# A two-layer graph network in f32: four node tiles instead of six in the first phase, and another place in memory for s of layer 1

## The chip, the cores and the metric

The kernel runs on one core of one Trainium2 chip. The metric is the device time of one execution in microseconds (us). The kernel before takes 2101.34 us, the median of three runs (2098.91 to 2105.48). A core has five engines with an order of instructions each: TensorE (PE, with its weight loads PEld), VectorE (DVE), ScalarE (ACT), GpSimd (POOL) and SyncE (SP). Transfers are issued by SP, ACT and POOL.

## The reference

There are 4096 nodes with 512 features in f32 and one dense matrix `adj` of 4096 × 4096, in which about 0.8% of the entries are not zero. Both layers begin with a layer norm and a relu, and add their result to their input.

```python
# layer 0
h = relu(layernorm(x))
d = where(adj.sum(1) > 0, adj.sum(1) ** -0.5, 0)
x = x + relu((d[:, None] * adj * d[None, :]) @ h @ W0 + b0)
# layer 1
h = relu(layernorm(x))
s, t = (h @ W1) @ a[:512], (h @ W1) @ a[512:]
e = leaky_relu(s + t.T, 0.2)
p, q = softmax(where(adj > 0, e, -1e12)), -softmax(where(adj > 0, -e, -1e12))
x = x + elu(concat(p @ h, q @ h) @ wtrans)
```

## The kernel before

The nodes are cut into 32 tiles of 128. Layer 0 computes `y = d * (h @ W0)` for all tiles (`y0`, kept in memory) and then `adj @ y`, for a few output tiles at a time: a group `(i0, n)` of the list `GROUPS` stands for the n output tiles from i0 on. For each of the 32 row tiles of y, a group needs a block of the transposed matrix, 128 rows × n·128 columns (`at`).

**The first group, (26, 6),** is worked on while y is made. In round j SP issues the four pieces of 512 KB of the rows of adj (`ar`, `load_adj`) and the block `at`. ACT sums three of the pieces and VectorE one (L669, L671), since d needs the sum of a row. POOL issues x, four tiles ahead (L640, five buffers). The layer norm (statistics on VectorE, L433; the root and the scaling on ACT, L632, L636) gives hx (two buffers); TensorE transposes it (L648), multiplies by W0 (yp, L679), and ACT scales by d (L702). Then come n products of 128 × 512 for row tile j (acc, L852), in n PSUM banks that stay occupied for the whole phase; transposes and projections alternate in the banks that are left of the eight. The pattern of non-zeros of the block goes as bytes to the tables of layer 1 (`pack`, L716 to L727). After 32 rounds, and four small products for the attention vectors, the phase is over.

**The later groups** use products of half width, 128 × 256. Two output tiles and two row tiles form a 2 × 2 block, and seven products of sums and differences take the place of eight (`multiply_blocks`, L893). The sums of columns are made by VectorE from `at` (`sum_at`, L880 to L883); the differences of y (`sum_y`, L865 to L868) are made once, in the first of these groups. A group has 16 steps jp. The results of a group are taken out of PSUM at the start of the next (`evict` after the first group, with three extra tiles in `new_y` since it has six rows; `join_blocks` after the others), and its rows are finished there, one in each of the first steps: relu and residual (L808), layer norm (h, L636, two buffers), two dot products with the attention vectors (`prod`, L816), and the row is written to eight tables of layer 1 (`put_row`, L443: one write issued by POOL, seven by ACT, 258 KB each). At step 8, TensorE turns the values s of these rows (`spread_s`, L831), and ACT writes them out. The rows of the last two groups are written to one table and copied to the others later. The order of instructions on each engine comes from a planner; some are pinned to the order of the program. `EARLY` says in which group the masks of the last three are packed, since these must be there when layer 1 begins. The lists of neighbours for layer 1 are made beside the groups (`make_lists`).

**Layer 1** gathers for each pair of tiles the rows of the neighbours from a table (POOL, L451), adds s and t (`scores`, L463), takes the two exponentials, multiplies by the mask (L482), and multiplies (L1296); then comes the product with wtrans (L1319). Its tiles are laid out by pools in the order in which these are opened; what lies where the late products of layer 0 read must wait for them. s is loaded by SP (L1256), wtrans by ACT.

Of the kernel before, what the change touches and what calls it, by code (L numbers as in the profile page):

```python
# [8 lines left out]
F32 = mybir.dt.float32  # L9
# [10 lines left out]
P = 128  # L20
IB = 512


GROUPS = ((26, 6), (16, 4), (20, 4), (0, 4), (4, 4), (8, 4), (12, 4), (24, 2))

EARLY = {(24, 2): (2,), (12, 4): (3,), (8, 4): (4,)}
PAIR0 = 16
Y_PARTS = (8, 11, 13)
T_PARTS = (7, 9)
# [230 lines left out]
def gcn_gat_kernel(  # L260
# [24 lines left out]
    N, F = x.shape  # L285
# [15 lines left out]
    TT = RPT * RB // P  # L301
    late0, n_late = GROUPS[-1]
    tab0 = PAIR0 // TT
# [14 lines left out]
    with sbuf(name="init", bufs=1) as init:  # L318
        column = init.tile([P, P], F32, name="column")
        nc.vector.memset(column[:, 0:1], 0.0)  # L320
        n = 1
# [195 lines left out]
    with sbuf(name="y0", bufs=1) as y_pool, sbuf(name="wa", bufs=1) as wa_pool, sbuf(name="bits", bufs=4) as bits_pool, sbuf(name="small0", bufs=4) as small, ExitStack() as rest, ExitStack() as lists:  # L517
# [16 lines left out]
        keys, lst = {}, {}  # L534
# [214 lines left out]
        def affine(y, acc, j):  # L749

            nc.vector.scalar_tensor_tensor(y, acc, d_all[:, j : j + 1], b_bc, ALU.mult, ALU.add)
            return y

        def new_y(work, j, k):
            if k < 0:
                return work.tile([P, F], F32, tag="y", name=f"y{j}", bufs=4)
            if k == 0:
                spare.append(make_pool.tile([P, 3, F], F32, tag="keys", name="spare"))
            return spare[0][:, k]

        def evict(i0, acc, work, _):

            return {
                i0 + k: affine(new_y(work, i0 + k, k - 3), a, i0 + k) for k, a in enumerate(acc)
            }

        def join_blocks(i0, n, acc, work, new_w):

            ys = {}
            for x in range(n // 2):  # L770
                p16, p23, p45, p7 = acc[x]
                j0, j1 = i0 + x, i0 + n // 2 + x
                ys[j0], ys[j1] = y, v = [new_y(work, j, -1) for j in (j0, j1)]
                w = new_w(f"w{j0}")[:, :H]
                nc.vector.tensor_copy(y[:, :H], p16[:, :H])
                nc.vector.tensor_tensor(w, p16[:, H:], y[:, :H], ALU.add)  # L776
                nc.vector.tensor_tensor(y[:, H:], p45[:, H:], w, ALU.add)

                def first(p23=p23, y=y):
                    nc.vector.tensor_tensor(y, p23, y, ALU.add)  # L780

                def second(p7=p7, w=w, p45=p45, v=v):
                    two = "p (a f) -> p a f"
                    nc.vector.tensor_tensor(w, p7, w, ALU.add)
                    nc.vector.tensor_tensor(
                        v.rearrange(two, a=2),
                        p45.rearrange(two, a=2),
                        w.unsqueeze(1).to_broadcast([P, 2, H]),
                        ALU.add,
                    )  # L790

                if n == 2:
                    first()
                    affine(y, y, j0)
                    second()
                    affine(v, v, j1)
                else:
                    second()
                    first()
            if n > 2:  # L800
                for j, y in ys.items():
                    affine(y, y, j)
            return ys

        def finish0(work, j, y, h, prod):
# [15 lines left out]
            put_row(nc.gpsimd, tab0, j, h)  # L821
            if all(not j0 <= j < j0 + n for j0, n in GROUPS[-2:]):
                for g in others:
# [97 lines left out]
        i0, n = GROUPS[0]  # L921
        with sbuf(name="w0", bufs=1) as w0_pool, sbuf(name="ain", bufs=9) as ain, sbuf(name="xs", bufs=5) as x_pool, sbuf(name="at6", bufs=5) as at_pool, sbuf(name="bits6", bufs=3) as bits6, sbuf(name="ln", bufs=3) as ln_pool:
# [39 lines left out]
            acc = [bank(f"acc{i0 + k}") for k in range(n)]  # L962
            for j in range(NJ):
# [18 lines left out]
                pack(bits6, i0, j, ats.pop(j), j < 2)  # L982
                mark()
        pending = (GROUPS[0], partial(evict, i0, acc))
        listing, joining, spare = [], [], []

        def make_lists(g):
            make_keys(g)

            def rows_and_joins(c):  # L990
                count_listed(g, c, lst[g])
                li = table_rows(g, c, lst[g])
                joining.extend(partial(join, g, li, m) for m in range(c * NE, (c + 1) * NE))
                if c == 2:
                    joining.append(partial(deal, g))

            for n, (c, r) in enumerate(steps):
                listing.append(partial(list_round, keys[g], lst[g], n))
                if n == 5:
                    listing.append(partial(make_places, g))  # L1000
                if r + 1 == CAPS[c] // 8:
                    listing.append(partial(rows_and_joins, c))

        def judge():
# [25 lines left out]
            return verdict  # L1030

        def group(b, work, at_pool, sum_pool, step, prod, n_h=2):

            nonlocal pending
            i0, n = GROUPS[b]
            nj = 8 // n
            (p0, pn), take = pending
            order = [p0 + k for k in ((0, 2, 1, 3) if b > 1 else range(pn))]
            ats, sums = {}, {}

            def prepare(jp):
                if 2 * jp % nj == 0:
                    ats[jp] = load_at(at_pool, i0, n, 2 * jp, nj)
                    sums[jp] = sum_at(sum_pool, ats[jp], n, f"sums{i0}_{jp}")
                else:
                    ats[jp], sums[jp] = ats[jp - 1], sums[jp - 1]
                if b == 1:
                    sum_y(jp)

            prepare(0)  # L1050
            for j in order[:2]:
                if j not in xrs:
                    load_xr(j)
            for jp in range(NP):
                if jp + 1 < NP:
                    prepare(jp + 1)
                mark()
                if jp == 0:
                    ys = take(work, prod)
                    p7 = bank(f"p7_{i0}")  # L1060
                    acc = [
                        [*(bank(f"p{k}_{i0 + x}") for k in (16, 23, 45)), p7[:, x * H : (x + 1) * H]]
                        for x in range(n // 2)
                    ]
                multiply_blocks(acc, n, jp, ats[jp], sums[jp])
                if (i0, n) not in EARLY:
                    pack(bits_pool, i0, 2 * jp, ats[jp])
                for (e0, m), when in EARLY.items():
                    if b in when:
                        pack(bits_pool, e0, 2 * jp, load_at(at_pool, e0, m, 2 * jp, 2))  # L1070
                if jp < pn:
                    j = order[jp]
                    h = work.tile([P, ROW_W], F32, tag="h", name=f"h{j}", bufs=n_h)
                    finish0(work, j, ys.pop(j), h, prod)
                    if jp + 2 < pn:
                        load_xr(order[jp + 2])
                if jp == 8:
                    spread_s(p0, pn)
                if jp == NP - 4:
                    for k in (0, n // 2):  # L1080
                        load_xr(i0 + k)
                step(jp)
            pending = (GROUPS[b], partial(join_blocks, i0, n, acc))

# [5 lines left out]
        make_pool = lists.enter_context(sbuf(name="make", bufs=1))  # L1090
        with sbuf(name="work0", bufs=2) as work, sbuf(name="sums", bufs=3) as sum_pool, sbuf(name="at", bufs=6) as at_pool:

            def prod(name):
                return work.tile([P, F], F32, tag="q", name=name, bufs=1)

            for b in range(1, len(GROUPS) - 1):

                def step(jp):
                    if jp == 2 and b in (3, 5):
                        make_lists((1, 0)[b == 5])  # L1100
                    for _ in range((2, 3)[b == 6] if jp != 2 else 0):
                        if listing:
                            listing.pop(0)()
                    if joining:
                        joining.pop(0)()

                group(b, work, at_pool, sum_pool, step, prod)
            while listing:
                listing.pop(0)()
            while joining:  # L1110
                joining.pop(0)()
# [7 lines left out]
        with sbuf(name="work2", bufs=2) as work, sbuf(name="sums2", bufs=2) as sum_pool, sbuf(name="at2", bufs=4) as at_pool, sbuf(name="scratch", bufs=1) as scratch, sbuf(name="pair", bufs=1) as pair:  # L1119
# [98 lines left out]
            k = late0 % EJ  # L1218
# [17 lines left out]
    def sparse_layer1():  # L1236
        with ExitStack() as pools:

            def pool(name, bufs):
                return pools.enter_context(sbuf(name=name, bufs=bufs))  # L1240
# [2 lines left out]
            slots = ((0, 0), (1, 0), (1, 2), (1, 1), (0, 1), (0, 2))  # L1243
            g_pools = {s: pool("g%d%d" % s, 1) for s in slots}
            tmp, small, p_pool = pool("tmp", 1), pool("small1", 2), pool("p", 3)
            work, ut_pool, wt_pool = pool("work1", 2), pool("ut", 2), pool("wt", 1)
            warm = small.tile([P, 1], F32, tag="warm", name="warm", bufs=1)
            nc.scalar.activation(warm, sign, AF.Exp)
            wt_sb = wt_pool.tile([P, 2 * FC, F], F32, name="wt_sb")
            s_pool = pool("s", 2)  # L1250
            gath, wgt, us, uts, srow = {}, {}, {}, {PAIR0: ut0}, {}

            def load_s(k):
# [82 lines left out]
            order = [r for n in pairs for r in (2 * n, 2 * n + 1)]  # L1336
# [86 lines left out]
```

## Time and profile before

| what | us |
|---|---|
| median of three runs | 2101.34 |
| the profiled execution | 2098.72 |
| its span, first to last instruction | 2096.8 |
| TensorE busy (95% of the span) | 1996.2 |
| VectorE busy (53%) | 1120.1 |
| POOL busy (44%) | 917.0 |
| ACT busy (24%) | 511.3 |
| products of the first phase (acc, L852), 384 records | 174.9 |
| projections (yp, L679), 256 records | 123.2 |
| half-width products of layer 0 (L893), sum of its four rows | 880 |

A record is one entry of the profile; an f32 product shows as two. Busy time counts an engine's instructions without the ones that issue transfers. The mean granted clock of TensorE is 0.981. In the timeline, the first product of the first phase starts at 25.80. The groups start at 334.33 (16, 4), 433.4 (20, 4), 530.6 (0, 4), 637.9 (4, 4), 758.2 (8, 4), 866.0 (12, 4) and 975.1 (24, 2), and the last of them ends at 1030.4. TensorE is busy 200.0 of every 200 us from 1200 to 2000, in layer 1.

### The profile page before, as it was taken

What the parts mean: (1) busy time and instruction counts of PE and PEld (TensorE: products, weight loads), DVE (VectorE), ACT (ScalarE), POOL (GpSimd) and SP (SyncE); (2) the same over time, 40 slices, a digit from 0 to 9 for tenths busy, and PEclk for the clock granted to TensorE, in tenths of its full rate; (3) what the DMA queues carried; (4) which work ended last, traced back from release to release, by engine and by line L of the source; (5) the groups of instructions that cost most, each with busy time, mean ns of one, the idle gap of its engine ahead of it and who ended that gap; (6) DMA issues with size and microseconds to landing.
All of it is one profiled execution on the core that took longest, in us unless ns stands there. A gap on an engine that the chain in (4) does not pass through costs nothing.

```text
span 2096.8 us, 20037 instructions
## 1 busy us (share of the span) xinstructions
PE 1996.2 (95%) x6456; PEld 1180.1 (56%) x6456; DVE 1120.1 (53%) x2805; ACT 511.3 (24%) x876; POOL 917.0 (44%) x980
## 2 busy tenths in 40 slices
PE   7999999999899879899879999999999999999998
PEld 3444446888787768788634444444444444444443
DVE  5444436563798458945545455554544544445441
ACT  4645612222332310000111222212212211121120
POOL 2010001111113320220577777777777777776740
PEclk9999999999999999999989999999999999999999
DMA  9988927887887776383689888888888888888850
GB/s 381 366 307 321 371 71 252 290 284 220 307 281 256 253 222 238 90 270 111 204 265 302 255 288 293 263 287 254 271 240 274 261 258 245 242 247 236 240 161 22
DMA packets 188040, 524.11 MB, mean 250 GB/s; under 512 B 25235, under 2 KB 34419, under 8 KB 187926
## 3 DMA queue, kind: packets, MB, share of 16 engines
q0 software_dynamic: 71296, 275.22, 42.2%
q1 hardware_dynamic: 86640, 192.78, 27.1%
q10 hardware_dynamic: 29990, 54.75, 7.4%
q8 instruction: 52, 0.85, 0.2%
q14 instruction: 62, 0.51, 0.1%
HBM read 430.83 MB, written 102.92 MB: 255 GB/s over the span
## 4 chain that ended last, share of the span: by engine, by line
PE 49%; DVE 6%; DMA 5%; POOL 3%; issue 2%; ACTq 1%; ACT 0%; DVEq 0%; SPq 0%; POOLq 0%
PE u L1296 32%; PE o L1319 10%; PE p L893 5%; POOL g L451 3%; DMA g<-table,idx 2%; DVE keys L393 1%; PE tp L508 1%; DVE lst L391 1%; DMA table<-h 1%; DMA ld<-li,off 1%; DMA at<-in_adj_t 1%; PE u L1174 1%; ACTq L443 1%; DVE prod L816 0%; DMA table<-m 0%
## 5 line engine op out<-in xcount | busy, mean ns | idle before, releaser
L451 POOL DMA_INDIRECT g<-table,idx x704 | 747.8, 1062 | 259.9 <-issue 186.4
L1296 PE MATMUL u<-g,p 128*128 128x512 f32 x1736 | 762.4, 596 | 9.8 <-DVE p L482 9.8
L1296 PEld LDWEIGHTS u<-g,p 128*128 128x128 f32 x1736 | 326.0, 191 | 397.5 <-issue 362.9
L463 DVE TENSOR_TENSOR z<-g,s 128x512 f32<-128x512 f32 (+1 forms) x124 | 77.5, 625 | 390.4 <-DMA g<-table,idx 357.8
L893 PE MATMUL p<-t,sums 128*128 128x256 f32 x832 | 249.0, 384 | 13.3 <-DVE sums L881 13.3
L893 PE MATMUL p<-y,sums 128*128 128x256 f32 x832 | 252.0, 385 | 6.5 <-DVE sums L883 6.5
L893 PE MATMUL p<-y,at 128*128 128x256 f32 x832 | 252.4, 386 | 4.9 <-DMA at<-in_adj_t 4.6
L1319 PE MATMUL o<-wt_sb,ut 128*128 128x512 f32 x512 | 225.1, 592 | 0.5 <-ACT ut L512 0.5
L473 ACT ACTIVATE p<-z 128x896 f32<-128x896 f32 (+2 forms) x136 | 116.1, 905 | 268.3 <-DVE z L469 248.1
L893 PEld LDWEIGHTS p<-t,sums 128*128 128x128 f32 x832 | 159.6, 193 | 37.5 <-DVE sums L881 15.5
L893 PEld LDWEIGHTS p<-y,sums 128*128 128x128 f32 x832 | 160.7, 193 | 29.9 <-DVE sums L883 7.3
L852 PE MATMUL acc<-y,at 128*128 128x512 f32 x384 | 174.9, 593 | 2.4 <-ACT y L702 2.4
L482 DVE SCALAR_TENSOR_TENSOR p<-g,p 128x384 f32<-128x384 uint8 (+1 forms) x256 | 143.2, 620 | 63.3 <-ACT p L473 62.3
L893 PEld LDWEIGHTS p<-y,at 128*128 128x128 f32 x832 | 159.3, 193 | 30.7 <-ACT m L716 5.0
L727 POOL DMA_DIRECT2D table<-m x71 | 54.3, 766 | 248.5 <-ACT m L716 145.5
L1319 PEld LDWEIGHTS o<-wt_sb,ut 128*128 128x128 f32 x512 | 94.8, 190 | 107.8 <-issue 106.9
L716 ACT ACTIVATE m<-at 128x1024 uint8<-128x1024 f32 (+1 forms) x110 | 105.2, 987 | 183.8 <-DMA at<-in_adj_t 137.3
L893 PE MATMUL p<-t,at 128*128 128x256 f32 x416 | 126.3, 386 | 18.5 <-DVE w L776 17.7
L1305 ACT ACTIVATE us<-u,rl 128x512 f32<-128x512 f32 x62 | 42.5, 686 | 414.7 <-issue 217.4
L679 PE MATMUL yp<-w_sb,hx_t 128*128 128x512 f32 x256 | 123.2, 627 | 17.3 <-ACT y L702 14.8
L852 PEld LDWEIGHTS acc<-y,at 128*128 128x128 f32 x384 | 70.5, 190 | 80.5 <-issue 77.4
L413 POOL DMA_INDIRECT ld<-li,off x48 | 43.2, 901 | 159.8 <-DMA ld<-li,off 115.8
(182 smaller groups left out, 1718.5 us busy)
## 6 DMA issues: line engine op xcount, KB each, us to landing
at<-in_adj_t SPq DMA_DIRECT2D x136, 512.0 KB, 5.1
ar<-in_adj SPq DMA_DIRECT2D x128, 512.0 KB, 8.4
table<-h ACTq DMA_DIRECT2D x182, 258.0 KB, 5.8
table<-m POOLq DMA_DIRECT2D x55, 256.0 KB, 5.6
at<-in_adj_t SPq DMA_DIRECT2D x32, 384.0 KB, 5.0
g<-table,idx POOLq DMA_INDIRECT x704, 4.3
xr<-in_x SPq DMA_DIRECT2D x32, 256.0 KB, 3.5
x<-x1d SPq DMA_DIRECT2D x32, 256.0 KB, 5.2
```

The costliest lines, as they stand in the source:

```text
L413: return nc.gpsimd.indirect_dma_start(out=lst_dram[g][:, :], out_offset=bass.IndirectOffsetOnAxis(ap=off[g][:, e, c : c + 1], axis=0), in_ ...
L451: nc.gpsimd.indirect_dma_start(out=gt[:, k, :], out_offset=None, in_=table[2 * n // RPT], in_offset=bass.IndirectOffsetOnAxis(ap=idx[n // ...
L463: return nc.vector.tensor_tensor(z, t.to_broadcast([P, n, RB]), s.unsqueeze(1).to_broadcast([P, n, RB]), ALU.add)
L473: i = nc.scalar.activation(p[:, :, g, :], z, AF.Exp, scale=(1.0, -1.0)[g])
L482: nc.vector.scalar_tensor_tensor(e, m, 0.0, e, ALU.is_gt, ALU.mult)
L679: nc.tensor.matmul(yp, hx_t[j][:, c * P : (c + 1) * P], w0_sb[:, c, :], start=c == 0, stop=c == FC - 1,)
L716: nc.scalar.activation(m, at, AF.Sign)
L727: nc.gpsimd.dma_start(out=rows_of(t, e)[:, c:, ROW_W + (a - t * TT) * P // 4 : ROW_W + (b - t * TT) * P // 4], in_=masks[i0][:, c:, (a - i ...
L852: nc.tensor.matmul(a, at[:, 0, it * P : (it + 1) * P], y0[j], start=j == 0, stop=j == NJ - 1)
L893: i = nc.tensor.matmul(out, left[:, x * P : (x + 1) * P], right, start=jp == 0 and first, stop=jp == NP - 1 and (final or not first),)
L1296: nc.tensor.matmul(u, p[:, k0 + k].rearrange("p g c -> p (g c)"), gt[:, k, :F].bitcast(F32), start=k0 + k == 0, stop=k0 + k == nk - 1,)
L1319: nc.tensor.matmul(po, ut[:, g, c, :], wt_sb[:, g * FC + c, :], start=g == 0 and c == 0, stop=g == 1 and c == FC - 1,)
```

## The change

The list of groups is cut in another way: the first phase has the four tiles 28 to 31, and tiles 26 and 27 become a group of half-width products of their own, third in the list. The indexes that name groups go up by one, so that masks and lists are made in the same groups as before. A group of two reads `at` in blocks of four row tiles, so its masks are packed once for two steps, and its two rows are finished in plain order. The eviction of the first phase needs no extra tiles. In layer 1 the pool of s is opened ahead of that of wtrans, so in each partition s lies 16 KB lower and wtrans 4 KB higher.

```diff
-GROUPS = ((26, 6), (16, 4), (20, 4), (0, 4), (4, 4), (8, 4), (12, 4), (24, 2))
+GROUPS = ((28, 4), (16, 4), (26, 2), (20, 4), (0, 4), (4, 4), (8, 4), (12, 4), (24, 2))
 
-EARLY = {(24, 2): (2,), (12, 4): (3,), (8, 4): (4,)}
+EARLY = {(24, 2): (3,), (12, 4): (4,), (8, 4): (5,)}
...
-        def new_y(work, j, k):
-            if k < 0:
-                return work.tile([P, F], F32, tag="y", name=f"y{j}", bufs=4)
-            if k == 0:
-                spare.append(make_pool.tile([P, 3, F], F32, tag="keys", name="spare"))
-            return spare[0][:, k]
+        def new_y(work, j):
+            return work.tile([P, F], F32, tag="y", name=f"y{j}", bufs=4)
 
         def evict(i0, acc, work, _):
 
             return {
-                i0 + k: affine(new_y(work, i0 + k, k - 3), a, i0 + k) for k, a in enumerate(acc)
+                i0 + k: affine(new_y(work, i0 + k), a, i0 + k) for k, a in enumerate(acc)
             }
...
-            order = [p0 + k for k in ((0, 2, 1, 3) if b > 1 else range(pn))]
+            order = [p0 + k for k in ((0, 2, 1, 3) if b > 1 and pn == 4 else range(pn))]
...
-                if (i0, n) not in EARLY:
+                if (i0, n) not in EARLY and 2 * jp % nj == 0:
                     pack(bits_pool, i0, 2 * jp, ats[jp])
...
-                    if jp == 2 and b in (3, 5):
-                        make_lists((1, 0)[b == 5])
-                    for _ in range((2, 3)[b == 6] if jp != 2 else 0):
+                    if jp == 2 and b in (4, 6):
+                        make_lists((1, 0)[b == 6])
+                    for _ in range((2, 3)[b == 7] if jp != 2 else 0):
...
-            work, ut_pool, wt_pool = pool("work1", 2), pool("ut", 2), pool("wt", 1)
+            work, ut_pool, s_pool, wt_pool = pool("work1", 2), pool("ut", 2), pool("s", 2), pool("wt", 1)
...
             wt_sb = wt_pool.tile([P, 2 * FC, F], F32, name="wt_sb")
-            s_pool = pool("s", 2)
```

More of the change, by code (lines that the diff above doesn't have):

```diff
@@ L772, in join_blocks @@
                 j0, j1 = i0 + x, i0 + n // 2 + x
-                ys[j0], ys[j1] = y, v = [new_y(work, j, -1) for j in (j0, j1)]
+                ys[j0], ys[j1] = y, v = [new_y(work, j) for j in (j0, j1)]
                 w = new_w(f"w{j0}")[:, :H]
@@ L984, in gcn_gat_kernel @@
         pending = (GROUPS[0], partial(evict, i0, acc))
-        listing, joining, spare = [], [], []
+        listing, joining = [], []
         def make_lists(g):
```

## The prediction

> **What bounds the kernel now.** I read the page first: the engine totals, the 40 slices and the chain of work that ended last. Then I cut the first 350 us into windows, listed the waits of that stretch and of the groups behind it, and followed TensorE and ACT along the timeline. From the page, busy time and the slices of TensorE, its granted clock and the DMA engines:
>
> ```profile
> PE 1996.2 (95%) x6456; PEld 1180.1 (56%) x6456; DVE 1120.1 (53%) x2805; ACT 511.3 (24%) x876; POOL 917.0 (44%) x980
> ...
> PE   7999999999899879899879999999999999999998
> ...
> DMA  9988927887887776383689888888888888888850
> ```
>
> TensorE is the bound over the whole span, but the first five slices (262 us) are also the ones with the fullest DMA engines. There two limits lie close together, which the windows show (columns: window, length, busy us and count of PE, PEld, DVE, ACT, POOL, then clock, DMA share, GB/s):
>
> ```profile
> 50.00:100.00 50.00, 47.31 (x124) 21.20 (x123) 24.78 (x81) 29.80 (x64) 4.35 (x7) 1.00 0.98 366
> ...
> 250.00:300.00 50.00, 50.00 (x135) 23.16 (x134) 16.08 (x40) 16.96 (x32) 3.01 (x4) 1.00 0.48 165
> ```
>
> TensorE is busy for 45 to 47 of each 50 us while the DMA engines are 0.85 to 0.98 busy, and only after 250, when the last row of adj has been fetched, is it never idle. The waits of the first 350 us name what stops it (waited for, us, times, longest):
>
> ```profile
> DVE sta L433 <- DMA xt<-in_x: 96.4, 23, 7.9
> ...
> PE yp L679 <- ACT y L702: 14.8, 6, 4.7
> ```
>
> A projection waits for y of the row tile before, because two PSUM banks are left beside six accumulators and alternate between transposes and projections. y waits for its row sum and its place in VectorE's order, where 23 statistics of the layer norm stand waiting for x. TensorE's gaps between its first acc (25.80) and the group (16,4) (334.33) add up to 16.2 us. Undisturbed, one row tile takes it 9.02 us (the projections stand at 272.20 and 281.22):
>
> ```profile
> 272.20 3.60 PE L679 MATMUL yp<-w_sb,hx_t 128*128 128x512 f32 x8
> 275.63 2.74 PE L852 MATMUL acc<-y,at 128*128 128x512 f32 x6
> 278.21 0.60 PE L648 MATMUL tx<-ident,hx 128*128 128x128 f32 x4
> 278.64 2.74 PE L852 MATMUL acc<-y,at 128*128 128x512 f32 x6
> 281.22 3.60 PE L679 MATMUL yp<-w_sb,hx_t 128*128 128x512 f32 x8
> ```
>
> **The skill.** "DMA: Bandwidth & Descriptors", Specifications, gives about 358 GB/s as the memory's limit for a core; the trace agrees, with 366 to 379 at a share of 0.98 and 0.99, so the row tiles cannot be fetched faster. "PSUM — Partial Sum Buffer", Specifications, counts 8 banks of 512 f32 per partition: six accumulators leave two, four leave four. "TensorE: Matmul & The Clock Gate", What's actually happening, says that an idle window halves the clock until TensorE has been busy for a while: here the clock is 0.5 for 6.8 us after the gap of 8.64 at 697.28, some 2 us more per such gap.
>
> **The change part by part.** All against the profiled execution, 2098.72 us (span 2096.8 and 1.9 around it), which lies 2.6 below the median of 2101.34.
>
> Removed: two full products per row tile, 64 in all. A product is two records, and eight records of the projection take 3.43 (275.63 − 272.20), so 0.429 a record: 64 × 0.858 = 55.0 us. The step becomes 9.02 − 4 × 0.429 = 7.30. Traffic per row tile falls from 2.85 MB (rows of adj 2.10, columns 0.39, x 0.26, masks 0.10) to 2.69 (columns 0.26, masks 0.07), at 366 GB/s 7.3 us. So both limits now meet. If the 16.2 us of waits stay, the phase ends 55.0 earlier: (16,4) starts at 279.3, a mean step of 7.8 from 25.8 (with 3.6 for the weight rows at the end). The row sums allow it: the last is taken at 263.5 now, and from there to the first half-width product lie some 4 us to the last y and 28 differences of y and 4 sums of columns on VectorE, 0.335 each by their spacing, 10.7: 278.
>
> Added: the group (26,2), 16 steps × 7 half-width products × 2 records = 224 records. Four of those take 0.86 us (334.33 to 335.19 below), so 0.2155 each: 48.3 us. The same form stands at the end now: (24,2) takes 55.3 with 4.2 us of gaps and some half clock.
>
> ```profile
> 334.33 0.59 PE L893 MATMUL p<-y,at 128*128 128x256 f32 x2
> 334.76 0.59 PE L893 MATMUL p<-t,sums 128*128 128x256 f32 x2
> 335.19 0.59 PE L893 MATMUL p<-t,at 128*128 128x256 f32 x2
> ```
>
> Moved: the rows of a group are finished inside the next. (16,4) now finishes four rows instead of six, which ends its wait of 1.8 us for the sixth (1.8, once, in the waits of s_ps): −2. The rows of (16,4) are finished in the short group, and there the product that turns s (s_ps, L831) comes in step 10. Counted along TensorE's new order it is reached 32.4 us after the group's start, and needs the fourth row. How fast four rows come is seen in (20,4), which starts at 433.4 (ACT; x7 are the writes of one row to seven tables):
>
> ```profile
> 440.93 0.81 ACT L636 ACTIVATE h<-y,rrb 128x512 f32<-128x512 f32 x1 [0.46 <-DVE rrb L633]
> ...
> 460.00 9.89 ACTq L443 DMA_DIRECT2D table<-h  x7
> 470.00 0.81 ACT L636 ACTIVATE h<-y,rrb 128x512 f32<-128x512 f32 x1 [9.39 <-DMA table<-h]
> ```
>
> The fourth h is 36.6 after the start and its dot product about 39. In the new ACT order the seven writes of the second and of the third row stand together ahead of the fourth h, as h has two buffers; I put the dot product at +40 to +43. TensorE waits 7.5 to 11 for it, and all products of the later steps are queued behind: I take 9, and 2 for the half clock afterwards. At the good end nothing is waited for (rows 7 us earlier), at the bad end twice as much; both stay in the range. The two rows of (26,2) are finished in (20,4), where four fitted: nothing.
>
> s of layer 1: its load is issued at 1064.61, when the late products have read what lay there, and lands some 5.5 later. VectorE uses s first at 1075.05, and that subtraction waited for the gathered rows:
>
> ```profile
> 1075.05 0.69 DVE L463 TENSOR_TENSOR z<-g,s 128x512 f32<-128x512 f32 x1 [5.83 <-DMA g<-table,idx]
> ```
>
> So s has about 5 us of slack, and moving it forward gains nothing. The output weights move by 4 KB in its place; they land at 1106, 12 us ahead of their first use (1118.85): nothing. The mask packing of the new group is 8 packs of a form that the other groups have: nothing while ACT and the mask queue keep their idle time. The three extra tiles of the eviction go, with their first wait: nothing.
>
> Sum: −55.0 − 2 + 48.3 + 9 + 2 + 0 = +2.3, so 2101.0 for an execution like the profiled one, and with the 2.6 to the median 2103.6: **2104**.
>
> **The rivals.** *The first phase gets stuck at its fetches (slower).* x(j) is fetched when hx four or five tiles before frees its buffer; then come the transfer (about 6 us), the statistics, the root on ACT, hx. Between hx 6 and hx 15 (42.1 and 133.3) this goes at 10.1 us a tile, more than TensorE's 9.02. The new order lets the loop span two tiles, which I estimate at 7.6; if it comes out half way to the mean step of now (9.5), 8.5, (16,4) starts at 25.8 + 31 × 8.5 + 4 = 293: 14 us later than in my sum, 2118. From 7.95 a tile on, this decides for slower by over 0.3%. For it speaks the DMA share of 0.98; against it, that the windows 100 to 200 have 309 to 319 GB/s, room to catch up.
>
> *Freed banks (faster).* With four spare banks a projection no longer waits for y just before: the 14.8 us vanish, and the phase falls to TensorE's floor, 25.8 + 32 × 7.30 + 3.6 = 263, with the row sums and the differences of y at the earliest at 265 to 268. That is 11 to 14 us earlier, 2090 to 2093. The fetches need at least 88.7 MB / 366 = 242 us, which allows it. Against it: waits for banks were only where the fetches' delay showed.
>
> *The writes clog (slower).* 28 row writes of 258 KB and 14 more masks fall into 48 us instead of 97. If the fourth row comes at +50 or the fetches of the next columns queue behind, the stall is 18 to 20 and the next group opens with a gap as those at 697 and 875 (8.6 and 8.3, with half clock): +15, 2119.
>
> **How the numbers follow.** A difference under 0.3% (6.3 us) can't be told from none. My sum 0.35 (no change 0.22, slower 0.10, faster 0.03); stuck at the fetches 0.27 (slower 0.24, none 0.03); freed banks 0.22 (faster 0.20, none 0.02); clogged writes 0.16 (slower 0.15, none 0.01). Together faster 0.23, none 0.28, slower 0.49. The likeliest single case is the sum, 2104, alone 2096 to 2112. The range takes in the floor with a small stall (2083) and the two slow cases partly together (2128).
>
> **What would show it.** Right: (16,4) starts at 275 to 283 in the new profile; s_ps of its rows has a wait of 7 to 11 for the dot product in the short group, which takes 57 to 62 us; the projections in the first phase still wait for y; s lands earlier and the first subtraction after the gather still waits for its rows. A start near 265 speaks for the freed banks, near 293 for the fetches; a gap over 15 us in the short group, or a new one at the start of (20,4), for the writes. Wrong altogether I would be if the later groups, whose order and columns only move, gained or lost gaps of several us each: from (20,4) on they have 42 us of them now, which I left as they are.

## The result and the profile after

The changed kernel takes 2087.87 us, the median of seven runs (2084.48 to 2094.75), where the kernel before takes 2101.34 (seven runs, 2098.07 to 2106.61): a ratio of 0.9935, with an interval of 0.9916 to 0.9955. It is faster by 13.5 us. I had put 2104 and held slower for the likelier side. The profiled executions, 2098.72 and 2087.87, have spans of 2096.8 and 2086.1, 10.7 apart.

The page of the changed kernel, the same lines as before:

```profile
PE 1990.7 (95%) x6554; PEld 1198.1 (57%) x6554; DVE 1131.6 (54%) x2851; ACT 520.4 (25%) x885; POOL 918.0 (44%) x980
...
PE   7999999899998889899879999999999999999998
...
DMA  9999785876977876464689888888888888888850
```

TensorE has 5.5 us less to do, about the 6.7 that the count of products says. The other half of the 10.7 is idle time of TensorE that is gone. The windows of the first phase (length, busy us and count of PE, PEld, DVE, ACT and POOL, clock, DMA share, GB/s):

```profile
50.00:100.00 50.00, 47.12 (x128) 21.32 (x127) 26.32 (x81) 32.39 (x69) 4.42 (x8) 1.00 0.97 358
100.00:150.00 50.00, 49.62 (x137) 23.12 (x136) 26.37 (x84) 33.03 (x72) 4.84 (x9) 1.00 1.02 390
...
250.00:300.00 50.00, 49.11 (x177) 32.01 (x176) 35.12 (x107) 15.63 (x22) 7.39 (x15) 1.00 0.69 240
```

The window 100 to 150 had 309 GB/s before and has 390 now. The waits of the first 300 us (us, times, longest) show that VectorE still waits for x, but no projection waits for y any more (14.8 us before); in their place stand short waits of acc (2.4 us before):

```profile
DVE sta L433 <- DMA xt<-in_x: 73.0, 22, 5.2
...
PE acc L848 <- ACT y L702: 7.7, 7, 2.4
```

The end of the phase and the new wait in the short group, from TensorE's timeline:

```profile
264.34 7.13 PE L848 MATMUL acc<-y,at 128*128 128x512 f32 x16
271.99 0.67 PE L889 MATMUL p<-y,at 128*128 128x256 f32 x2 [0.52 <-DMA at<-in_adj_t]
...
407.86 0.59 PE L827 MATMUL s_ps<-ident,s_all 128*4 128x128 f32 x2 [5.35 <-DVE prod L812]
```

Where the time went, stretch by stretch, from the starts of the groups in the two timelines. Idle is TensorE's idle time in the stretch, "half" its time at half clock:

| stretch | before | idle, half | after | idle, half | difference |
|---|---|---|---|---|---|
| until (16, 4) starts | 334.3 | | 272.0 | | −62.3 |
| (16, 4) | 99.1 | 1.8, 0 | 98.0 | 0.4, 0 | −1.1 |
| (26, 2) | | | 56.4 | 5.4, 6.8 | +56.4 |
| (20, 4) | 97.2 | 0, 0 | 97.2 | 0, 0 | 0 |
| (0, 4) | 107.3 | 6.5, 6.8 | 100.0 | 1.3, 0 | −7.3 |
| (4, 4) | 120.3 | 17.7, 13.7 | 124.6 | 21.1, 21.9 | +4.3 |
| (8, 4), (12, 4), (24, 2) | 272.5 | 18.9, 23.8 | 271.0 | 16.9, 25.9 | −1.5 |
| to layer 1's first product (L1296) | 47.9 | | 46.5 | | −1.4 |
| from there to the end | 1018.3 | | 1020.4 | | +2.1 |

Three lines ask for a reason: the first phase gained 62.3, not 55.0; the short group cost 56.4, not 59.3; and (0, 4), whose own work the change leaves as it was, became 7.3 shorter.

The first phase can be taken apart. From its first acc to the start of (16, 4), TensorE's gaps sum to 16.2 us before and 10.2 after, and its time at half clock is 13.7 and 3.2. The 62.3 are thus 57.4 less of busy time (some 55 for the products taken out, about 2.4 for the clock) and 6.0 less of gaps, less 1.1 because the first acc starts later (26.92 for 25.80). The same instructions ran again in other profiles, with only later groups or layer 1 changed: (16, 4) starts at 271.8 (e1), 274.7 (e5) and 273.8 (e13) beside the 272.0 here, and at 338.4 (e2) and 337.1 (e16) beside the 334.3 before. A difference of 3 or 4 us between two single profiles of this phase is therefore no finding.

### The profile page after: what moved, and what is told of

Its sections match the earlier page's. It is cut to its first block, busy times and chain, and to the rows that moved or that the text cites. A ratio compares the mean times of both kernels' runs of the same rounds, so it can differ in the third digit from the quotient of the medians.

```text
span 2086.1 us, 20403 instructions
## 1 busy us (share of the span) xinstructions
PE 1990.7 (95%) x6554; PEld 1198.1 (57%) x6554; DVE 1131.6 (54%) x2851; ACT 520.4 (25%) x885; POOL 918.0 (44%) x980
## 3 DMA queue, kind: packets, MB, share of 16 engines
q1 hardware_dynamic: 90864, 192.78, 27.4%
## 4 chain that ended last, share of the span: by engine, by line
PE 56%; DVE 4%; DMA 3%; POOL 2%; issue 1%; ACT 0%; ACTq 0%; DVEq 0%; POOLq 0%
PE u L1291 35%; PE o L1314 11%; PE p L889 8%; POOL g L451 1%; PE tp L508 1%; DVE keys L393 1%; DMA at<-in_adj_t 1%; DVE lst L391 1%; DMA ld<-li,off 1%; PE u L1170 1%; DMA g<-table,idx 1%; DMA table<-h 0%; PE cs L498 0%; DMA table<-m 0%; ACT m L716 0%
## 5 line engine op out<-in xcount | busy, mean ns | idle before, releaser
L889 PE MATMUL p<-t,sums 128*128 128x256 f32 x896 | 268.4, 384 | 15.3 <-DVE sums L877 15.3
L889 PE MATMUL p<-y,at 128*128 128x256 f32 x896 | 272.2, 386 | 4.4 <-DMA at<-in_adj_t 4.2
L889 PE MATMUL p<-y,sums 128*128 128x256 f32 x896 | 271.7, 385 | 1.3 <-DVE sums L879 1.3
L889 PEld LDWEIGHTS p<-t,sums 128*128 128x128 f32 x896 | 172.1, 193 | 41.3 <-DVE sums L877 17.5
L889 PEld LDWEIGHTS p<-y,at 128*128 128x128 f32 x896 | 171.7, 193 | 32.4 <-ACT m L716 4.0
L889 PEld LDWEIGHTS p<-y,sums 128*128 128x128 f32 x896 | 173.2, 194 | 26.5 <-DVE sums L879 1.7
L716 ACT ACTIVATE m<-at 128x1024 uint8<-128x1024 f32 (+1 forms) x118 | 113.9, 994 | 222.8 <-DMA at<-in_adj_t 176.5
L1314 PEld LDWEIGHTS o<-wt_sb,ut 128*128 128x128 f32 x512 | 94.8, 190 | 107.8 <-issue 107.1
L889 PE MATMUL p<-t,at 128*128 128x256 f32 x448 | 136.3, 387 | 19.2 <-DVE w L772 19.1
L876 DVE TENSOR_TENSOR sums<-at 128x256 f32<-128x256 f32 x112 | 47.2, 421 | 167.5 <-PE p L889 124.8
L848 PE MATMUL acc<-y,at 128*128 128x512 f32 x256 | 122.4, 604 | 7.7 <-ACT y L702 7.7
```

Of the source, the lines that this page charges most:

```text
L716: nc.scalar.activation(m, at, AF.Sign)
L848: nc.tensor.matmul(a, at[:, 0, it * P : (it + 1) * P], y0[j], start=j == 0, stop=j == NJ - 1)
L876: op(t[:, 0], a[:, :, 0, 1], a[:, :, 1, 1], ALU.add)
L889: i = nc.tensor.matmul(out, left[:, x * P : (x + 1) * P], right, start=jp == 0 and first, stop=jp == NP - 1 and (final or not first),)
L1314: nc.tensor.matmul(po, ut[:, g, c, :], wt_sb[:, g * FC + c, :], start=g == 0 and c == 0, stop=g == 1 and c == FC - 1,)
```

## The experiments

Most of them ran on chips where the kernel before takes 2132 to 2135 us, about 1.5% more, chiefly in (24, 2) and layer 1; so times are compared as ratios to the runs of the kernel before on the same chip. For stretches on these chips, e1 stands for the changed kernel and e2 for the kernel before; up to (12, 4) they differ little between chips (107.4 in e2 and 107.3 for (0, 4)).

**The place of s.** e1 takes the second part of the change back, e2 does it alone:

```diff
-            work, ut_pool, s_pool, wt_pool = pool("work1", 2), pool("ut", 2), pool("s", 2), pool("wt", 1)
+            work, ut_pool, wt_pool = pool("work1", 2), pool("ut", 2), pool("wt", 1)
             wt_sb = wt_pool.tile([P, 2 * FC, F], F32, name="wt_sb")
+            s_pool = pool("s", 2)
```

> The change without its second part: the new groups, but s of layer 1 stays where it was. If s has slack, as I reckoned (about 5 us), it takes what the whole change takes: 2088, ratio to before 0.993 to 0.994, and the first product of layer 1 starts as long after the end of layer 0 as with the whole change (46.5 us). If the place of s brings part of the gain, it is 2090 to 2094 and that stretch is 1 to 5 us longer.

> The kernel before with only s moved. If s has slack: ratio 1.000 within 0.001, the load of s is issued earlier than 1064.6, and the first subtraction still waits for gathered rows. If s was late: 0.5 to 5 us faster, and the stretch from the end of layer 0 to the first product of layer 1 (47.9) shrinks by as much.

e1: ratio 0.9936 (0.9911 to 0.9961), the same as the whole change's 0.9935. e2: 1.0001 (0.9986 to 1.0016). The absolute times expected do not apply on this chip. Whatever the place of s is worth, it is within the 0.15% of e2's interval; and the first product of layer 1 comes 40.7 us after layer 0 in e1, where s stays, and 40.4 and 40.3 in e3 and e4, where it is moved. The timelines of the changed kernel (SP, then VectorE) show that it does what it says, all the same:

```profile
1018.80 0.79 SPq L1251 DMA_DIRECT2D s<-sd  x2
1062.25 0.69 DVE L463 TENSOR_TENSOR z<-g,s 128x512 f32<-128x512 f32 x1 [4.59 <-DMA g<-table,idx]
```

The load is issued 46 us earlier than before (1064.61), 34 of them counted from the end of layer 0, and the subtraction waits for the gathered rows as it did.

**Banks or traffic.** e3 occupies two PSUM banks through the first phase, e4 fetches six tiles of columns and uses four.

```diff
             acc = [bank(f"acc{i0 + k}") for k in range(n)]
+            hold = [bank(f"hold{k}") for k in range(2)]
+            for hb in hold:
+                nc.tensor.matmul(hb[0:1, 0:1], y0[0][:, 0:1], ones[:, 0:1], start=True, stop=False)
...
+            for k, hb in enumerate(hold):
+                nc.tensor.matmul(hb[0:1, 0:1], y0[NJ - 1][:, 0:1], ones[:, 0:1], start=False, stop=True)
+                nc.vector.tensor_copy(held[:, k : k + 1], hb[0:1, 0:1])
```

```diff
-                    ats[j + 1] = load_at(at_pool, i0, n, j + 1, 1)
+                    ats[j + 1] = load_at(at_pool, i0 - 2, n + 2, j + 1, 1)[:, :, 2 * P :]
```

> The changed kernel with two PSUM banks occupied through the first phase (two one-column products into each, nothing else), so two are left to alternate between transposes and projections, as before. If the freed banks gave the 7 us that the first phase gained beyond the removed products: (16, 4) starts at 278 to 281 instead of 272, projections wait for y again for some 10 us in sum, and the time is 2094 to 2096. If the smaller traffic gave them: (16, 4) starts at 271 to 274, the time stays at 2088 to 2090.

> The changed kernel, where each load of columns in the first phase fetches six node tiles as before and the products use four of them: 0.13 MB more per row tile, 4.2 MB in all, the banks as in the change. If the traffic bounds the phase: the row sums end 8 to 12 us later than the 249 of the changed kernel, (16, 4) starts at 280 to 284, and the time is 2096 to 2100. If the banks are what counts: (16, 4) starts at 272 to 275, the time is 2088 to 2091.

e3: (16, 4) starts at 278.1 against 271.8 in e1, and the ratio is 0.9958 (0.9946 to 0.9971). Against the four profiles of the changed kernel's first phase (271.8 to 274.7), the freed banks are thus worth 3.4 to 6.3 us of the gain, by a single profile of e3; the two ratios are 0.0022 apart, 4.7 us, but their intervals overlap. VectorE and ACT had the same order in the first phase as in the changed kernel. In the waits of e3 the old line is back:

```profile
PE yp L679 <- ACT y L702: 10.9, 7, 3.8
```

e4 had a ratio of 1.0126 (1.0092 to 1.016), far more than either theory allowed: (16, 4) started at 315.5. Yet the DMA engines had room, as its windows show:

```profile
100.00:150.00 50.00, 40.06 (x102) 17.77 (x101) 19.09 (x61) 23.25 (x51) 3.46 (x6) 0.95 0.80 280
150.00:200.00 50.00, 40.91 (x100) 18.09 (x98) 17.98 (x60) 22.29 (x48) 3.46 (x6) 0.91 0.79 281
```

The planner had moved the instructions. In the steady rounds of the changed kernel, VectorE takes the statistics of tile 22 after the row sum of 15; in e4 those of tile 23. So e4 is no clean test of the traffic. Its waits point to something else:

```profile
POOL xt L640 <- ACT hx L636: 151.4, 19, 11.3
ACT rs L694 <- DVE rs L693: 114.0, 30, 6.7
DVE sta L433 <- DMA xt<-in_x: 94.7, 28, 6.0
```

That reads as a loop: hx frees a buffer, POOL fetches x, VectorE waits for it with its statistics, and the row sums, ACT's roots and y wait behind.

**The loop through x.** e6, e7 and e8 give x seven buffers instead of five and fetch it six tiles ahead, on the kernel before, the changed one and e4.

```diff
-                if j + 4 < NJ:
-                    load_x(x_pool, nc.gpsimd, j + 4)
+                if j + 6 < NJ:
+                    load_x(x_pool, nc.gpsimd, j + 6)
```

> The kernel before with seven buffers for x and its fetches six tiles ahead instead of four; in the steady rounds the order of every engine is the same but for the statistics, which are those of two tiles further on. If the fetch of x is part of a loop (hx frees the buffer, fetch, statistics ahead of the row sums on VectorE, root, y, hx) that stops TensorE: the gaps of 16 us in the first phase go, (16, 4) starts at 318 to 324 instead of 334 to 338, ratio 0.993 to 0.995. If two spare PSUM banks alone make the waits: it starts where it did, ratio 1.000.

> The changed kernel with the same seven buffers for x. If the loop through x still costs something: (16, 4) starts at 264 to 268 instead of 272, ratio to before 0.990 to 0.992. If the loop is no longer a limit with four spare banks: 271 to 273, ratio 0.9935.

> Six columns fetched, four used, with seven buffers for x; otherwise in the order of the run with six columns. If the 43 us of that run came from the loop through x and not from 4.2 MB more traffic: (16, 4) starts at 275 to 285 instead of 315.5, ratio 0.994 to 0.998. If they came from the traffic: it stays at 310 to 316, ratio 1.011 to 1.013.

| | ratio, interval | (16, 4) starts at |
|---|---|---|
| e6, before | 1.0013 (1.0002 to 1.0023) | 336.5 (338.4 in e2) |
| e7, changed | 0.9912 (0.9888 to 0.9936) | 270.7 |
| e8, six columns | 1.0102 (1.0082 to 1.0121) | 311.2 |

By what I had written, the loop was refuted in e6 and e8; e7 has the start of one case and the ratio of the other. But the planner had put the statistics two tiles further on, so VectorE waited for the newest x as before; in e6:

```profile
DVE sta L433 <- DMA xt<-in_x: 89.1, 21, 7.8
```

More buffers had only moved the loop. It is opened by holding the statistics back. e9, e10 and e11 do that, on the same three kernels, by keeping them and VectorE's row sums in the order of the program:

```diff
-            normalize(hx, xs.pop(j), f"a{j}", pin)
+            normalize(hx, xs.pop(j), f"a{j}", True)
...
-                if pin:
+                if pin or c == 1:
                     tc.keep_in_program_order(i)
```

> The kernel before, where VectorE's statistics of x are kept in the order of the program among its row sums: in steady rounds those of tile 17 stand behind the row sum of 15, where those of tile 20 stood ahead of it. x is fetched as before. The run with seven buffers moved the statistics along with the fetches, so it left the loop closed; this one opens it. If VectorE waiting for x is what makes y late: the wait of the statistics (96 us) falls below 30, TensorE's gaps of 16 us go, (16, 4) starts at 318 to 325 instead of 334 to 338, ratio 0.992 to 0.995. If y is late for another reason: the start stays within 3 us, ratio 0.999 to 1.001.

> The same order of the statistics in the changed kernel. If the wait for x still costs there: (16, 4) starts at 263 to 268 instead of 272, ratio to before 0.989 to 0.992. If four spare banks have made it harmless, or the row fetches bound the phase by now: 270 to 273, ratio 0.993 to 0.9945.

> Six columns fetched, four used, with the statistics in the same order. If the 43 us of the run with six columns came from VectorE's wait for x that closes the loop: (16, 4) starts at 275 to 285 instead of 315.5, ratio 0.995 to 0.999. If from the 4.2 MB themselves, or from a loop through the buffers of the rows and columns: 305 to 316, ratio 1.008 to 1.013.

| | ratio, interval | (16, 4) starts at |
|---|---|---|
| e9, before | 0.9906 (0.9869 to 0.9944) | 316.4 |
| e10, changed | 0.9870 (0.9842 to 0.9897) | 261.3 |
| e11, six columns | 0.9875 (0.9846 to 0.9904) | 260.6 |

The ratios of all three lie below what I had put even for the better case, and all three start earlier, too. The wait of the statistics for x is gone from the lists of all three. The list of e9 begins:

```profile
POOL xt L640 <- ACT hx L636: 125.7, 17, 14.3
PEld acc L852 <- issue: 76.7, 318, 0.9
DVE m L718 <- DMA at<-in_adj_t: 67.2, 20, 8.7
```

POOL waits for hx as before, but nobody waits for POOL. In e10 and e11 TensorE is never idle from 50 to 250. The windows of e11:

```profile
100.00:150.00 50.00, 50.00 (x137) 23.35 (x136) 27.94 (x85) 33.19 (x70) 5.27 (x9) 1.00 1.03 405
150.00:200.00 50.00, 50.00 (x139) 23.52 (x137) 27.98 (x83) 33.14 (x69) 5.26 (x9) 1.00 1.01 389
```

Three things follow. The statistics' place on VectorE, ahead of row sums and waiting for x, was the cause of TensorE's gaps in the first phase, before and after. (The edit holds statistics and row sums in one order, so the two are shown together, not apart.) With the statistics held back, the 4.2 MB more traffic cost nothing (260.6 against 261.3). And with the waits gone, the two phases are 316.4 − 261.3 = 55.1 us apart: the 55.0 of the count. e10 is faster than both kernels.

**The turn of s in the short group.** e5 puts it five steps later.

```diff
-                if jp == 8:
+                if jp == (13 if b == 2 else 8):
                     spread_s(p0, pn)
```

> The changed kernel, where the product that turns s (s_ps) for the rows of (16, 4) comes five steps later in the short group (26, 2). If its wait for the fourth row's dot product (5.35 us, and half clock behind it) is on the path: the short group lasts 48 to 50 us instead of 56.4, 6 to 8 us less in all, ratio to before about 0.990. If the late rows hold up something else on VectorE in its place (its order has that dot product ahead of the sums of columns for the last steps): the gap moves to a product that waits for the sums, and the time stays within 2 us of the changed kernel.

Neither case as written, though the time is that of the second. The short group fell to 48.9 with no gap, 8.0 less than e1's 56.9; then (0, 4) took 109.1, where e1 has 100.4. Ratio 0.9942 (0.9927 to 0.9957). Its waits of TensorE from 370 to 630:

```profile
PE p L889 <- DVE sums L879: 8.2, 2, 6.4
```

That is the gap that the kernel before has in (0, 4). The changed kernel, e1, e3, e4, e7, e8, e10 and e11, all with the stall in the short group, do not have it: there (0, 4) takes 99.1 to 102.7. The same list from the start of (20, 4) to the end of (0, 4), in the kernel before and in the changed one:

```profile
PE p L893 <- DVE sums L883: 6.5, 2, 6.0
```

```profile
PE p L889 <- DVE sums L879: 1.3, 1, 1.3
```

Those sums stand on VectorE behind the dot product of a row, and this one waited for its h. The rows are late from the first one on: in ACT's order, packings of masks that wait for their columns stand ahead of it, and its h comes 14.5 us after the start of (0, 4) in the kernel before, 15.9 in e5 and 9.2 in the changed kernel. e12 makes such a stall in the kernel before, by the turn of the first six rows one step earlier, in (16, 4):

```diff
-                if jp == 8:
+                if jp == (7 if b == 1 else 8):
```

> The kernel before, with the product that turns s of the first six rows one step earlier in (16, 4), so that TensorE has to wait some 6 us longer there, in the group ahead of (20, 4), as the changed kernel does in its short group. If such a stall lets the fetches of columns get ahead and so takes away the gap in (0, 4) (6.5 us and half clock behind it): (16, 4) lasts 105 to 108 instead of 99, (0, 4) 99 to 103 instead of 107, ratio 0.999 to 1.001. If the gap in (0, 4) has nothing to do with it: (0, 4) still lasts 107, ratio 1.003 to 1.004.

(16, 4) took 107.3 with 7.3 idle, and (0, 4) still 108.2: ratio 1.0049 (1.0027 to 1.0071). A stall there is paid, and nothing comes back. Next I suspected ACT's seven row writes behind both the wait of s_ps and the gap; e13 gives three of them to POOL, e14 joins this with e10 and e5, and e15 does it on e9.

```diff
-                for g in others:
-                    put_row(nc.scalar, g, j, h)
+                for k, g in enumerate(others):
+                    put_row(nc.gpsimd if k > 3 else nc.scalar, g, j, h)
```

> The changed kernel with three of the seven row writes of a node tile issued by POOL instead of ACT. If the writes on ACT's queue are behind both the wait of s_ps in the short group and the gap of (0, 4): the fourth row of (16, 4) comes 10 us earlier, the short group lasts 48 to 51 us instead of 56.4, (0, 4) lasts 97 to 101 (the gap does not come back as it did when only the turn of s was moved), the columns are issued further ahead, and the ratio to before is 0.986 to 0.990. If POOL's own work (masks, x1, writes) takes the place of ACT: the short group lasts 54 to 60 and the ratio stays at 0.993 or above. If the gap of (0, 4) has another cause: short group 49, (0, 4) 107 to 109, ratio 0.9935.

> The changed kernel with the statistics in program order, the turn of s five steps later in the short group, and three of seven row writes on POOL: all three causes taken away. If they add up: (16, 4) starts at 261, the short group lasts 48.5, (0, 4) 97 to 101, (4, 4) less than 115; ratio to before 0.977 to 0.983. If the gaps of the later groups only move on: 0.985 to 0.987, as with the statistics alone.

> The kernel before with the statistics in program order and three of seven row writes on POOL: the groups as they were. If, with the waits gone, the change is worth its count of products alone (55.0 us removed, 48.3 added): this takes 6 to 8 us more than the run with all three on the changed kernel, 0.3% more. If the change needs the waits to be worth something: the two are equal within 2 us.

These three ran on a chip where the kernel before takes 2102.29. e13: 1.0009 (1.0000 to 1.0018), short group 57.2, (0, 4) 109.3; by the numbers this is my second case, that POOL's work takes the place of ACT's, but the trace below gives another reason. e14: 0.9913 (0.9896 to 0.9930), with the start of (16, 4) at 260.4 and the short group at 48.9 as foretold, but (20, 4) at 103.1 and (0, 4) at 110.3; a miss. e15: 1.0010 (0.9996 to 1.0024), with (16, 4) at 107.1 and (0, 4) at 117.7; it took 18.2 us more than e14, where I had put 6 to 8, or within 2: a miss. ACT's timeline in e13, at the third and fourth row, and TensorE's, at s_ps in the short group and at the gap in (0, 4):

```profile
393.81 0.81 ACT L636 ACTIVATE h<-y,rrb 128x512 f32<-128x512 f32 x1 [5.72 <-DMA table<-h]
...
403.13 0.81 ACT L636 ACTIVATE h<-y,rrb 128x512 f32<-128x512 f32 x1 [7.55 <-DMA table<-h]
...
405.52 0.59 PE L827 MATMUL s_ps<-ident,s_all 128*4 128x128 f32 x2 [5.40 <-DVE prod L812]
...
566.40 1.22 PE L889 MATMUL p<-t,sums 128*128 128x256 f32 x2 [7.96 <-DVE sums L877]
```

The fourth row did come sooner, 30.4 us after the group's start where the changed kernel has 35.3; it still waits for writes to leave one of the two buffers of h. The stall stayed because the planner had put s_ps earlier, too, behind 126 records of the group and not 150: TensorE stood there from 27.4 on, where it had been from 32.5 on. In (0, 4) the planner had put the fourth row's dot product ahead of seven operations of `sum_at` that stand ahead of it in the changed kernel, and the product after the gap waits for sums behind it. So these three runs changed the order along with the queue, and are no clean test of ACT's writes.

What helped was to set each fetch of columns against its use, SP's issue against TensorE's first product from it:

| fetch | changed | e5 | before | e12 | e16 |
|---|---|---|---|---|---|
| (20, 4), first | 387.5, 38.9 ahead | 390.1, 31.3 | 402.5, 30.8 | 411.8, 30.8 | 404.2, 30.8 |
| (20, 4), row tile 4 | 413.7, 24.8 | 410.6, 22.9 | 418.7, 26.8 | 427.7, 27.1 | 419.8, 27.3 |
| (0, 4), first | 502.2, 21.4 | 504.1, 14.5 | 514.4, 16.2 | 524.6, 15.3 | 516.2, 22.5 |

Up to the start of (20, 4) each issue follows TensorE at the same distance (30.8, as buffers come free), so the stall of e12 in (16, 4) delayed both. Within (20, 4) that distance shrinks: the issues go at a pace of their own. Counted from the start of the short group, the first fetch for (0, 4) comes at 132.2 in the changed kernel and at 131.5 in e5, although TensorE gets to (20, 4) 7.6 us earlier in e5. There a stall of TensorE is distance won, which (0, 4) would have lacked. What sets that pace is open. SyncE's own waits in (20, 4) give a lead: what came last was mostly the landing of an earlier load of columns (43.4 us in the kernel before, 55.9 in e5), then ACT's packing of masks (12.7 and 12.5); TensorE's products made 7.3 and 0.7. No run changes the loads alone. e16 tests TensorE's part by a stall in (20, 4) of the kernel before:

```diff
-                if jp == 8:
+                if jp == (4 if b == 2 else 8):
```

> The kernel before, with the product that turns s of the rows of (16, 4) put into step 5 of (20, 4), some 34 us after the group's start, where the fourth row's dot product (39 us) makes TensorE wait about 5 us. If the fetches of columns keep a clock of their own from here on and the gap in (0, 4) is what TensorE is ahead of them: (20, 4) lasts 103 to 106 instead of 97, the columns of (0, 4) are issued 20 to 23 us ahead of their use instead of 16, (0, 4) lasts 99 to 103 instead of 107, and the ratio is 0.999 to 1.001. If the gap in (0, 4) does not depend on that: (0, 4) lasts 106 to 109 and the ratio is 1.003 to 1.005.

All as the first theory has it: TensorE waits in (20, 4), which takes 103.7; the columns of (0, 4) are issued 22.5 ahead; (0, 4) takes 99.0; ratio 0.9997 (0.9984 to 1.0011). The other profiles agree: leaving out the three with shared writes, the six with 14.5 to 17.1 us of distance at (0, 4) have 5.4 to 8.2 us of gaps there, and the nine with 20.8 to 22.5 have 0.3 to 2.8. Distance alone does not do it: e13 has 21.6 and a gap of 8.0, by its order. The stall in e16's timeline:

```profile
474.04 0.38 PE L831 MATMUL s_ps<-ident,s_all 128*4 128x128 f32 x2 [4.75 <-DVE prod L816]
```

## Why the prediction was wrong

**"If the 16.2 us of waits stay".** They did not. This is the step that failed in the first phase: the term −55.0 measured −62.3. The gaps fell from 16.2 to 10.2, and the 13.7 us at half clock, which my sum left as they were without a word, to 3.2. The freed banks gave 3.4 to 6.3 of the missing 7.3 (e3); what gave the rest is not shown. I had this mechanism as a rival at 0.22, with the floor (263) as its price; the truth, 272.0, lies half way to it. My argument against the rival, that the waits for banks only show the delay of x, fits e9, where they go with the statistics held back and no bank freed. It was wrong as an argument, all the same: with two more banks the next projection no longer waits for y, so the same delay costs less. My second support, the row sums whose last is taken at 263.5 and so allow no start before 278, took for a limit of the fetches what the order of the instructions sets. The last is taken at 249.0 in the changed kernel and at 232.7 in e10, with the same rows fetched.

**"So the row tiles cannot be fetched faster."** Wrong. I took the 358 GB/s of the Trainium skill ("DMA: Bandwidth & Descriptors", Specifications) and the 366 of the trace for a ceiling; e10 and e11 had 404 and 405 over 50 us, and here the measurement decides. That table row is the rate of a memory stack halved for two cores, and this kernel runs on one. The profile before could have told me: my windows of 50 us had averaged over slower moments. Cut into forty slices of 7.5 us, its first 300 us show 401 to 417 GB/s in twelve of them:

```profile
GB/s 254 391 408 417 404 401 392 406 407 404 375 287 303 379 412 387 292 115 342 256 348 360 364 353 102 342 395 333 403 372 251 405 408 407 354 192 54 82 73 73
```

**The short group, 48.3 + 9 + 2.** The place and the cause were right: s_ps waits for the fourth row's dot product, in the short group. TensorE got there 32.5 us after the group's start, as counted. The wait was 5.35 and not 9, since the fourth h came at 405.25, 35.3 after the start, and its dot product was done at 37.8 and not at 40 to 43. The half clock lasts 6.8 us, of which 4.5 lie behind the wait; by my estimate that costs half as much, 2.2, near the 2 I had put. (At 697.28, too, only 3.2 of the 6.8 us lie behind the gap.) The stretch took 56.4 and not 59.3. ACT's timeline has the rows as I had read them from its order, the writes of two rows together ahead of the fourth h:

```profile
392.14 0.81 ACT L636 ACTIVATE h<-y,rrb 128x512 f32<-128x512 f32 x1 [3.04 <-DMA at<-in_adj_t]
392.25 0.81 ACTq L443 DMA_DIRECT2D table<-h  x2
393.09 12.11 ACTq L443 DMA_DIRECT2D table<-h  x12
405.25 0.82 ACT L636 ACTIVATE h<-y,rrb 128x512 f32<-128x512 f32 x1 [11.34 <-DMA table<-h]
```

**What comes after the stall.** I left the gaps of the later groups as they were, though I had named them as what would show me wrong; this is the other step that failed, and its size is the same, 7.3. In the changed kernel the stall of the short group gives (20, 4) and (0, 4) distance to their fetches, and (0, 4) saves 7.3; e5 and e16 show this in both directions. It is no law: the stall of e12 in (16, 4) bought nothing. In my sum the stall stood at +11; with what (0, 4) saves, it cost about nothing against the kernel before.

**The sum.** −62.3 − 1.1 + 56.4 − 7.3 gives −14.3, and the +3.5 of the other stretches (−10.7 in all, by the spans) is mostly (4, 4), a group that took between 120.3 and 125.8 over all the runs. Part of what (0, 4) saves may come back there: without the shared writes, (4, 4) took 123.6 on average where (0, 4) had the distance and 121.3 where it had not. The terms in which I was off are thus −7.3 in the first phase, −2.9 in the short group and −7.3 in (0, 4). Right were the counts (55.1 apart in e9 and e10; 64 × 0.858 is 54.9), −1.1 for the sixth row where I had −2, and 0 for s.

**The rivals.** The loop through x exists and is dear: e4 lost 43 us, and e11 wins them back by the order of VectorE alone, with the traffic of e4. I gave it 0.27 for this change, and the order that the planner chose for the statistics decided against it. I named the fetch of x as the thing that it gets stuck at, correctly, and the DMA share as evidence, wrongly: e4 had 0.80. My limit of 7.95 us a tile was off, too: with the formula beside it, it is 8.2. The clogged writes did not come.

## What to carry to other kernels

Where two engines run close together, waits need not stay when work is removed between them: ask what the removed work also occupied (here two banks), and price the wait again with that free. Before deeper buffers are given to a loop, look at where the consumer stands in its engine's order: an instruction that a planner puts as early as the buffers allow can wait just the same with more of them (96.4 us with five, 89.1 with seven), and holding it back brought the kernel with six tiles 0.9%, where the change brought 0.65%. Before a stall is removed, compare issue and use of the loads of the stretches behind it: where the issues keep their own pace, as here, the time can be lost again there. And when an experiment goes through a planner, compare the order of the instructions first: e4, e6 and e13 each moved more than their edit says.

## What the runs showed of the hardware

The DMA engines moved 404 and 405 GB/s over windows of 50 us, with the rows of adj (in pieces of 512 KB) making up most of it, where the kernel before at a share of 0.98 had moved 366: a share near 1 in one profile was not the most that can be moved. And the kernel before took 2102 us on one chip and 2132 to 2135 on three others.
